# A convolution-attention-expert kernel: a first block that loads and normalises one channel tile ahead of the other, a seam with operations issued in another order, and two stores from another queue

## The chip, the cores and the metric

The kernel runs on one core of a Trainium2 chip. The metric is the device time of one execution in microseconds; the kernel before took 1997.98 us as the median of three runs (1995.13 to 2001.15). One further execution was profiled and took 1985.54 us. Engines have short names: PE is TensorE (PEld its weight loads), DVE is VectorE, ACT is ScalarE, POOL is GpSimd and SP is SyncE, which only issues transfers. A name with a q behind it (ACTq, SPq) is an engine's sequencer, which issues the DMAs.

## The reference

Two images of 256 channels and 56x56 pixels go through two layers; cut to what matters:

```python
# layer 0
y = einsum('oc,bchw->bohw', w_qkv1, group_norm(x))        # 768 output channels
y = conv_general_dilated(y, w_qkv2, (1, 1), 'SAME', feature_group_count=768)   # 3x3, each channel alone
q, k, v = split(y)                                         # 8 heads of 32 channels
for s in (0, 1):                                           # 4 heads each, 7x7 window, dilation 1 and 2
    attn = softmax(q * scale . k over the window + rpb[s]) # bias by relative position
    outs[s] = attn . v
x = x + w_proj . concat(outs)
# layer 1, on 6272 tokens of 256
t = t + linear_attention(layer_norm(t))                    # elu+1 features, then a feed-forward block
t = t + experts(layer_norm(t))                             # top 2 of 8 experts, hidden 1024, gelu
```

group_norm takes mean and variance over 8 channels and all pixels, so no product can be scaled before a whole channel tile has been counted. 128 channels are one tile; x has two (ct 0 and ct 1), which are the two halves of the contraction of w_qkv1.

## The kernel before, in words

The work is a sequence of stages, each of which mixes two kinds of work, so that PE has something to do while the other waits.

- 0 to about 435 us: the convolutions of image 0 and its attention (`first_image`, L1064). `Convolutions.run` (L504) goes through six blocks of 128 output channels, each in two halves of 28 rows (hf 0 and 1). For each half: PE multiplies (`py`, L529, four row groups, two channel tiles each), ACT copies into a padded tile `ypad` (L535), and the 3x3 convolution follows. PE takes 8 of the 28 rows as nine diagonal matmuls (`pc`, L550). For the other 20 rows ACT does the first of nine taps (L569) and DVE the eight others (L579). The result `yc` lies in one of two buffers, and is stored to DRAM as `yd` (L587), from where the attention loads it again (`ld`, `v`).
- The head of that stage, the first 20 us: `load_x` (L462) loads x in four column pieces per channel tile, `norm_image` (L469) counts all of it (`bn_stats`, L478), adds up over groups with a small matmul by `g8` (`gps`), forms the scale with a power on POOL (L151), and DVE scales x in place (L499).
- Beside it `bias_tables` (L363) builds the attention's tables of exp(bias): a cleared tile `pf` is written to DRAM (`frame`), the biases are turned there element by element (`turned`, L374), put into the frame (L379), read back as `pf` (L383), ACT takes Exp (L387), POOL multiplies with masks (L405) and writes `fp`, from which the attention loads its tables `tab` (L714).
- 435 to about 746 us: the convolutions of image 1 as filling for half 0 of layer 1's linear attention (`linear`, L1659): `keys` (L267), then queries, messages, feed-forward and routing in an order of PE written out by hand.
- From about 746 us, the seam: the attention of image 1 begins, with the expert tiles of half 0 (`Experts.run`, L1601) as its filling. Before it, the last tokens of half 0 are stored (`store`, L1996) and routed: `weights` (L2033) takes an Exp on ACT, DVE finds slots (`chosen`, `before`, `slot`), POOL scatters token rows into `xs`. In the attention, `settle` (L772) copies transposed keys and queries (qT0, qT1, kT0, kT1) out of PSUM, `scores` (L641) takes Exp on ACT and multiplies it by a table on DVE, and `values` (L660) multiplies by v on PE. An expert tile gathers its tokens (`xr<-xs`, L1544), and `weigh` (L1567) forms their weights `eq` on DVE. `LEAD` is the number of steps by which the filling starts ahead.
- After about 1030 us: linear attention of half 1, then experts alone, with PE nearly always busy, to the end.

Every engine runs its instructions in order. A scheduler orders them from priorities and an estimate of when their inputs come; `tc.issue_after(x)` keeps an instruction behind x in that order, `tc.high_priority` moves it ahead, and `tc.manual_schedule` keeps the order as written for the engines it names. `anchors` is a dictionary of instructions that such orders refer to. Since one moved instruction shifts those around it, the order of every engine differs between the two kernels far behind the changed lines.

## Time and profile before

| | us |
|---|---|
| median of three runs | 1997.98 (1995.13 to 2001.15) |
| the profiled execution | 1985.54 |
| its span, first to last instruction | 1983.8 |
| PE busy | 1840.1 (93%) |
| DVE busy | 1093.3 (55%) |
| ACT busy | 705.8 (36%) |
| POOL busy | 578.8 (29%) |
| PE busy from 0 to 30, 30 to 75, 75 to 435 | 12.68, 42.68, 329.82 |
| PE busy from 435 to 746, 746 to 800, 800 to 1030 | 287.88, 40.10, 213.12 |
| PE busy from 1030 to 1960, 1960 to 1984 | 907.14, 6.66 |

The mean granted clock of PE is 0.972 of full speed; from 746 to 800 us it is 0.62. A line of the timeline in the next section reads: start, duration, engine, line of the kernel, operation, output<-inputs, shapes, count, and in brackets the idle time of the engine before it and what ended that.

### The profile page before, as it was taken

The numbers are of one execution on the slowest core, as the hardware profiler recorded it, in microseconds if no ns is written. First come the engines' busy times: TensorE is split into PE (matmuls) and PEld (weight loads), VectorE is DVE, ScalarE is ACT, GpSimd is POOL, SyncE is SP. The second block draws the span as 40 slices with busy tenths as digits, with TensorE's granted clock in tenths as the row PEclk, the third lists the DMA queues.
The fourth block names the chain that finished last, engine by engine and source line by source line (L and its number), as shares of the span: only waits on it lengthen the run. The fifth ranks groups of instructions, "written<-read, shape, count | busy, mean of one in ns | idle before, by whom it ended". The sixth has DMA issues, their size and how long they took to land.

```text
span 1983.8 us, 27692 instructions
## 1 busy us (share of the span) xinstructions
PE 1840.1 (93%) x9996; PEld 1304.7 (66%) x9996; DVE 1093.3 (55%) x2728; ACT 705.8 (36%) x1337; POOL 578.8 (29%) x634
## 2 busy tenths in 40 slices
PE   6999899988989997999989989999999999999996
PEld 3444454556645564665668755668788888888885
DVE  6887988889888546555557434655622222222121
ACT  2233324334434223544536543323322222222332
POOL 4520042025202444111126311345422323222221
PEclk9999999999989996999999999999999999999998
DMA  4644422350003334754464210114677676767995
GB/s 113 152 114 128 152 75 84 101 151 35 25 33 94 107 85 140 205 153 137 130 191 126 72 35 32 46 62 133 182 227 198 185 201 186 200 190 197 299 279 166
DMA packets 200147, 268.79 MB, mean 135 GB/s; under 512 B 30952, under 2 KB 158614, under 8 KB 199760
## 3 DMA queue, kind: packets, MB, share of 16 engines
q1 hardware_dynamic: 167920, 223.95, 37.4%
q0 software_dynamic: 19728, 27.54, 7.4%
q10 hardware_dynamic: 12352, 15.43, 2.3%
q8 instruction: 81, 1.33, 0.3%
q14 instruction: 66, 0.54, 0.1%
HBM read 200.19 MB, written 70.95 MB: 137 GB/s over the span
## 4 chain that ended last, share of the span: by engine, by line
PE 48%; DMA 5%; DVE 3%; ACT 3%; issue 1%; SPq 0%; POOL 0%; ACTq 0%; DVEq 0%; POOLq 0%
PE ph L1617 13%; PE py L1637 13%; PE p L1961 4%; DMA xr<-xs 2%; PE x L1637 2%; PE py L1977 2%; PE x L1617 2%; DMA xs<-in_c_fill 2%; PE po L666 2%; PE pm L1931 1%; PE kx L317 1%; PE x L359 1%; PE kp L305 1%; PE pq L1888 1%; PE px L1584 1%; PE s_ps L652 1%
## 5 line engine op out<-in xcount | busy, mean ns | idle before, releaser
L1617 PE MATMUL ph<-xe,w1e 128*128 128x256 f32 (+1 forms) x1448 | 309.2, 369 | 10.6 <-ACT hT L1621 4.1
L1637 PE MATMUL py<-w2e,hT 128*128 128x256 f32 x1392 | 311.3, 379 | 0.0
L1621 ACT ACTIVATE hT<-ph,sv 128x256 f32<-128x256 f32 (+1 forms) x362 | 165.7, 462 | 387.3 <-PE ph L1617 384.2
L1617 PEld LDWEIGHTS ph<-xe,w1e 128*128 128x128 f32 x1448 | 261.2, 190 | 49.8 <-ACT hT L1621 6.1
L1637 PEld LDWEIGHTS py<-w2e,hT 128*128 128x128 f32 x1392 | 260.1, 190 | 33.1 <-issue 0.2
L168 POOL DMA_INDIRECT y<-yt,idi x101 | 160.2, 1587 | 322.6 <-DVE yt L1643 178.2
L579 DVE SCALAR_TENSOR_TENSOR yc<-ypad,w,yc 128x1120 f32<-128x1120 f32 x144 | 202.5, 1410 | 31.4 <-ACT yc L569 29.0
L262 POOL TENSOR_TENSOR rs<-rs,mhalf 128x2 f32<-128x2 f32 (+3 forms) x90 | 72.8, 812 | 325.4 <-DVE rs L261 277.6
L529 PE MATMUL py<-x_sb,wq 128*128 128x448 f32 (+1 forms) x384 | 155.9, 538 | 8.3 <-ACT ypad L535 4.4
L656 ACT ACTIVATE p<-s_ps 112x952 f32<-112x952 f32 (+5 forms) x88 | 102.1, 1160 | 150.6 <-PE s_ps L652 101.4
L1574 DVE CAST idi<-xr 128x2 int32<-128x2 f32 (+1 forms) x53 | 10.9, 205 | 255.9 <-DMA xr<-xs 255.9
L657 DVE TENSOR_TENSOR p<-p,tab 112x952 f32<-112x952 f32 (+5 forms) x88 | 122.0, 1389 | 47.4 <-ACT p L656 47.3
L550 PE MATMUL pc<-ypad,diag 128*128 128x448 f32 x324 | 131.4, 547 | 0.0
L1643 DVE SCALAR_TENSOR_TENSOR yt<-py,eq,yt 128x256 f32<-128x256 f32 x87 | 41.7, 482 | 156.3 <-PE py L1637 156.1
L1599 POOL TENSOR_SCALAR yt<-b2e,eq 128x256 f32<-128x256 f32 x101 | 50.7, 507 | 257.6 <-DMA b2e<-in_L_ffn_b 198.6
L529 PEld LDWEIGHTS py<-x_sb,wq 128*128 128x128 f32 x384 | 72.2, 199 | 71.4 <-issue 55.7
L168 POOL DMA_INDIRECT xs<-row,si x98 | 97.5, 995 | 64.4 <-DVE si L2108 34.7
L572 DVE SCALAR_TENSOR_TENSOR yc<-ypad,w,yc 128x784 f32<-128x784 f32 x96 | 104.9, 1114 | 1.3 <-ACT yc L569 0.9
L666 PE MATMUL po<-p,v 98*32 98x170 f32 (+5 forms) x960 | 70.8, 376 | 28.6 <-DVE p L657 15.3
L550 PEld LDWEIGHTS pc<-ypad,diag 128*128 128x128 f32 x324 | 60.0, 191 | 52.3 <-issue 48.5
L1961 PE MATMUL p<-xT,fw 128*128 128x512 f32 (+1 forms) x208 | 93.6, 573 | 0.0
L1961 PE MATMUL p<-m2T,fw 128*128 128x512 f32 (+2 forms) x224 | 93.4, 539 | 0.0
(394 smaller groups left out, 2883.8 us busy)
## 6 DMA issues: line engine op xcount, KB each, us to landing
w1e<-in_L_ffn_W SPq DMA_DIRECT2D x53, 1024.0 KB
w2e<-in_L_ffn_W SPq DMA_DIRECT2D x53, 1024.0 KB
yd<-yc SPq DMA_DIRECT2D x24, 784.0 KB
ld<-yd SPq DMA_DIRECT2D x28, 448.0 KB
xr<-xs SPq DMA_DIRECT2D x48, 260.0 KB
b2e<-in_L_ffn_b SPq DMA_DIRECT2D x53, 128.0 KB
t<-td SPq DMA_DIRECT2D x12, 512.0 KB
y<-t ACTq DMA_DIRECT2D x24, 256.0 KB
```

What stands on the lines that cost most here:

```text
L168: ins = nc.gpsimd.indirect_dma_start(out=dst[:, :], out_offset=bass.IndirectOffsetOnAxis(ap=index, axis=0), in_=src, in_offset=None, **kw,)
L529: nc.tensor.matmul(py[:, :n, :], self.wq1[:, ct, oc * P : (oc + 1) * P], self.x_sb[:, ct, (q0 + g0) * WW : (q0 + g0 + n) * WW], start=(ct ...
L550: nc.tensor.matmul(pc, diag[:, tap, :], ypad[:, dy : dy + SHARE, dx : dx + WW], start=(tap == 0), stop=(tap == 8),)
L572: nc.vector.scalar_tensor_tensor(yc[:, y0:y1, :], src, w, yc[:, y0:y1, :], ALU.mult, ALU.add)
L579: nc.vector.scalar_tensor_tensor(yc[:, y0:y1, :], src, w, yc[:, y0:y1, :], ALU.mult, ALU.add)
L656: nc.scalar.activation(p[:nk, :, :n], s_ps[:nk, :, :n], AF.Exp)
L657: nc.vector.tensor_tensor(grid(p), grid(p), table[:nk], ALU.mult)
L666: nc.tensor.matmul(dst[hs] if w is None else den[hs], v[:nk, hs] if w is None else w[:nk, :], p[:, h, :, o : o + q.shape[2]], start=first ...
L1617: nc.tensor.matmul(p1, x.w1[:, ct, j * P : (j + 1) * P], x.xe[:, ct, :], start=(ct == 0), stop=(ct == 1),)
L1621: newest[3] = nc.scalar.activation(hT[:, j, :], p1, AF.Gelu, bias=x.sv[:, 4 + j : 5 + j]).ins
L1637: nc.tensor.matmul(py, hT[:, j, h * P : (h + 1) * P], x.w2[:, j, :], start=(j == 0), stop=(j == NJ - 1),)
L1961: nc.tensor.matmul(p1[:, :w], fw1[:, k, oc * P : (oc + 1) * P], rhs, start=(k == 0), stop=(k == 3))
```

## The change

It has three parts.

Head. A new function `first_block` takes the place of `load_x` and `norm_image` for image 0. x is loaded with all pieces of channel tile 0 first, from both queues in turn; after it come g8 and the first 128 columns of the weight, then channel tile 1; the rest of the weight comes later, from ACT's queue. Each channel tile is counted, normalised and scaled by itself, and the products of tile 0 for six of eight row groups are made while tile 1 is counted; they are kept in PSUM banks of the attention. The order on PE and DVE is written out there. The clearing of pf, and with it the writes of `frame` and `turned`, wait for the second statistic of channel tile 1; the loads of masks and of the projection weight come behind them.

Seam. In `keys` the addition of b2 on POOL is always made, and no longer in `message`. The weighing of an expert tile is put behind the newest multiplication by a table. The stores of tokens and the Exp in `weights` of half 0 are put behind the copies of kT1 of the attention's first group. `LEAD` goes from 22 to 24.

Stores. The two stores of `yc` of image 0, output block 1, are issued by ACT instead of SP.

```diff
-LEAD = 22
+LEAD = 24
...
-        if b2 is not None:
-            nc.gpsimd.tensor_tensor(t, t, b2[p].unsqueeze(1).to_broadcast([rows, n, C]), ALU.add)
+        nc.gpsimd.tensor_tensor(t, t, b2[p].unsqueeze(1).to_broadcast([rows, n, C]), ALU.add)
...
-            nc.vector.memset(pf, 0.0)
+            with tc.issue_after(anchors["counted"]), tc.high_priority():
+                nc.vector.memset(pf, 0.0)
...
-            nc.sync.dma_start(frame.rearrange("h r c -> (h r) c"), pf)
+            ld = nc.sync.dma_start(frame.rearrange("h r c -> (h r) c"), pf)
+            anchors.setdefault("framed", ld.ins)
...
-            with nc.allow_non_contiguous_dma(reason="676 values"):
+            with tc.issue_after(anchors["framed"]), nc.allow_non_contiguous_dma(reason="676 values"):
...
-            self.load_x(0)
             self.g8 = self.cw.tile([P, P], F32, name="g8")
-            nc.scalar.dma_start(self.g8, a["c_g8"])
+            self.wq1 = self.cw.tile([P, 2, 3 * C], F32, name="wq1")
+            wq1 = a["w_qkv1_t"].rearrange("(ct p) o -> p ct o", p=P)
+            for ct in range(2):
+                for k, (c0, c1) in enumerate(zip((0, G, 3 * G, 5 * G), (G, 3 * G, 5 * G, T))):
+                    eng = nc.scalar if k % 2 else nc.sync
+                    eng.dma_start(self.x_sb[:, ct, c0:c1], xv[0, :, ct, c0:c1])
+                if ct == 0:
+                    nc.scalar.dma_start(self.g8, a["c_g8"])
+                    nc.sync.dma_start(self.wq1[:, :, :P], wq1[:, :, :P])
...
+            nc.scalar.dma_start(self.wq1[:, :, P:], wq1[:, :, P:])
...
+        def first_block(self, att):
...
+            def mean(ct):
+                nc.vector.bn_aggr(mv[:, ct, :], st[:, ct, :, :].rearrange("p g s -> p (g s)"))
+                nc.tensor.matmul(gps[ct][:, 0:1], self.g8, mv[:, ct, 0:1], start=True, stop=True)
+                gm, dv = gms[ct], dvs[ct]
+                nc.vector.tensor_copy(gm, gps[ct][:, 0:1])
+                nc.vector.tensor_tensor(dv, mv[:, ct, 0:1], gm, ALU.subtract)
+                nc.vector.tensor_tensor(dv, dv, dv, ALU.mult)
+                nc.vector.tensor_tensor(dv, dv, mv[:, ct, 1:2], ALU.add)
...
+            with tc.manual_schedule(engines={mybir.EngineType.PE, mybir.EngineType.DVE}):
+                count(0, *range(NG))
+                mean(0)
+                variance(0)
+                count(1, 0)
+                scaled(0, 0, G)
+                products(0, 0)
+                count(1, 1)
+                scaled(0, G, T // 2)
+                products(0, 1)
+                count(1, *range(2, NG))
+                mean(1)
+                scaled(0, T // 2, T)
+                products(0, 2)
+                variance(1)
+                products(0, 3, 4, 5)
+                scaled(1, 0, G)
+                products(1, 0)
+                scaled(1, G, T // 2)
+                products(1, 1, 2)
+                scaled(1, T // 2, T)
+                products(1, 3, 4, 5)
...
-                    st = nc.sync.dma_start(
+                    st = (nc.scalar if (b, oc) == (0, 1) else nc.sync).dma_start(
...
-            nc.vector.tensor_tensor(grid(p), grid(p), table[:nk], ALU.mult)
+            anchors["scaled"] = nc.vector.tensor_tensor(grid(p), grid(p), table[:nk], ALU.mult).ins
...
+                                if banks and g == 0:
+                                    anchors["settled"] = ins.ins
...
-        next(tables)
         for k, (b, done) in enumerate(run):
+            if k == 0:
+                next(tables)
+                with tc.issue_after(anchors["framed"]):
+                    att.load_projection()
...
-                self.weigh(x)
+                with tc.issue_after(anchors["scaled"]):
+                    self.weigh(x)
...
-                if half == 0:
-                    tt = tk.at(n0 + k0, 2)
-                    nc.gpsimd.tensor_tensor(tt, tt, b2.unsqueeze(1).to_broadcast([P, 2, C]), ALU.add)
...
+        def behind():
+
+            turned = run == 0 and half == 0 and "settled" in anchors
+            return tc.issue_after(anchors["settled"]) if turned else nullcontext()
...
-                ins = nc.scalar.dma_start(
-                    y2[(n0 + k0) * P : (n0 + k0 + kn) * P, :].rearrange("(n p) c -> p n c", p=P),
-                    tk.at(n0 + k0, kn),
-                )
+                with behind():
+                    ins = nc.scalar.dma_start(
+                        y2[(n0 + k0) * P : (n0 + k0 + kn) * P, :].rearrange("(n p) c -> p n c", p=P),
+                        tk.at(n0 + k0, kn),
+                    )
...
-            with tc.issue_after(newest[3]) if half and newest[3] is not None else nullcontext():
+            with tc.issue_after(newest[3]) if half and newest[3] is not None else behind():
                 nc.scalar.activation(ms[1], ms[1], AF.Exp)
...
-                            tk, wk, sm, ps_a, bank, w_k, b2 if half or pairs[j][1] == 1 else None, kx, acc, *pairs[j], j == 0, j == len(pairs) - 1, j < 3 and half == 0
+                            tk, wk, sm, ps_a, bank, w_k, b2, kx, acc, *pairs[j], j == 0, j == len(pairs) - 1, j < 3 and half == 0
```

## The prediction

> **What bounds the kernel now.** I read the page first: its busy times and its chain.
>
> ```profile
> PE 1840.1 (93%) x9996; PEld 1304.7 (66%) x9996; DVE 1093.3 (55%) x2728; ACT 705.8 (36%) x1337; POOL 578.8 (29%) x634
> ...
> PE 48%; DMA 5%; DVE 3%; ACT 3%; issue 1%; SPq 0%; POOL 0%; ACTq 0%; DVEq 0%; POOLq 0%
> ```
>
> TensorE is busy for 1840.1 of 1983.8 us, so 143.7 us of it are gaps, and only these, or matmuls run at a low clock, can be won. The change touches the first 100 us and the seam near 750 us; so next the busy time of windows around the seam (columns: span, then busy time and count of PE, PEld, DVE, ACT, POOL, then granted clock, DMA share, GB/s):
>
> ```profile
> 735.00:747.00 12.00, 12.00 (x73) 8.32 (x63) 4.10 (x18) 3.19 (x11) 6.20 (x7) 1.00 0.47 126
> 747.00:760.00 13.00, 7.93 (x44) 6.14 (x42) 10.12 (x63) 4.78 (x17) 4.51 (x5) 0.63 0.28 79
> ...
> 781.00:798.00 17.00, 9.42 (x53) 4.97 (x56) 7.63 (x18) 4.61 (x7) 4.99 (x7) 0.60 0.79 271
> ```
>
> PE goes from fully busy to 61% and 55%, at a clock of 0.6. Then the timeline, for who releases whom. The head:
>
> ```profile
> 4.59 1.15 DVE L478 BATCH_NORM_STATS2 st<-x_sb 128x6 f32<-128x448 f32 x2 [3.58 <-DMA x_sb<-in_x]
> ...
> 9.89 1.03 SPq L374 DMA_DIRECT2D turned<-in_L_conv_rpb  x1
> 11.10 3.26 DVE L478 BATCH_NORM_STATS2 st<-x_sb 128x6 f32<-128x448 f32 x6 [1.11 <-DMA x_sb<-in_x]
> ...
> 17.92 4.50 DVE L499 TENSOR_SCALAR x_sb<-x_sb,gm,rs_gn 128x448 f32<-128x448 f32 x6 [0.85 <-POOL rs_gn L151]
> 18.49 8.14 PE L529 MATMUL py<-x_sb,wq 128*128 128x448 f32 x16 [1.62 <-DVE x_sb L499]
> ...
> 24.75 7.86 SPq L379 DMA_DIRECT2D frame<-turned  x2
> ...
> 28.41 11.33 DVE L579 SCALAR_TENSOR_TENSOR yc<-ypad,w,yc 128x1120 f32<-128x1120 f32 x8 [5.99 <-ACT yc L569]
> ...
> 33.60 2.38 SPq L383 DMA_DIRECT2D pf<-frame  x2
> ...
> 39.18 0.35 ACT L387 ACTIVATE pf<-pf 84x33 f32<-84x33 f32 x2
> ```
>
> Nothing multiplies before 18.49: x arrives until 11.1, then come statistics, normalisation, scaling. From 28.41 DVE runs taps almost without a pause to 68.05, so a later or earlier first tap carries on to there. The bias tables wait for two slow writes (the first is issued at 9.89, its reader leaves at 24.75). Times at which a transfer landed, here and below, are the ends of its packets in the trace's DMA records. The block that the third part moves:
>
> ```profile
> 72.19 1.23 ACT L569 ACTIVATE yc<-ypad,w 128x1120 f32<-128x1120 f32 x1 [8.46 <-DMA yd<-yc]
> ...
> 75.33 0.53 SPq L587 DMA_DIRECT2D yd<-yc  x1
> ...
> 81.45 1.23 ACT L569 ACTIVATE yc<-ypad,w 128x1120 f32<-128x1120 f32 x1 [1.21 <-DMA yd<-yc]
> ...
> 84.96 0.34 SPq L587 DMA_DIRECT2D yd<-yc  x1
> ```
>
> Two buffers hold yc; a new block waits until an old one is stored. The store issued at 75.33 could have gone when its taps ended (68.05), but stood behind table stores and loads on SP. The seam:
>
> ```profile
> 750.70 0.20 ACT L2037 ACTIVATE m<-m 128x4 f32<-128x4 f32 x1 [3.99 <-DVE m L2096]
> ...
> 751.39 1.75 PE L767 MATMUL x<-ident,ld 112*128 112x112 f32 x8 [3.76 <-ACT qT L776]
> ...
> 753.02 0.64 PE L2099 MATMUL x<-chosen,tri 128*128 128x32 f32 x2
> ...
> 786.37 0.23 DVE L1572 TENSOR_SCALAR eq<-xr,etmA 128x2 f32<-128x2 f32 x1 [5.72 <-DMA xr<-xs]
> ...
> 788.51 1.16 PE L666 MATMUL po<-p,v 112*32 112x280 f32 x8 [6.77 <-DVE p L657]
> ...
> 793.54 2.93 PE L1617 MATMUL x<-xe,w1e 128*128 128x256 f32 x6 [0.81 <-DVE xe L1587]
> ```
>
> Two gaps, 3.76 and 6.77 us. In the second, DVE stands in the expert weight eq, waiting for gathered tokens, while a finished softmax tile waits behind it for its table.
>
> **Part 1, the head.** Channel tile 0 of x comes first. All x lands from 4.6 to 11.6; at that pace half is there near 7.7. Its seven statistics (14 took 1.15+3.42+3.26 = 7.8, so 0.56 each) end at about 9.2. From the end of the aggregates to the first scaling took 17.92 - 14.81 = 3.1; so tile 0 is scaled from about 12.5 (9.2 + 0.26 + 3.1). DVE then has seven statistics (3.9) and two of the three scalings of tile 0 (1.1 of half of 4.50): 17.5. A second norm, 0.3 + 3.1, puts the scaling of tile 1 at 21.0 to 23.3. Scaling alone ends 0.9 later than before (22.42), but PE has done tile 0's six products by then; only the four of tile 1 in the first half remain for the first convolution, of which the last needs rows beyond column 1568, so it starts after 23.3. Its copy ends near 24.9 instead of 27.05; with the other copies and the 1.23 of ACT's first tap DVE starts its taps at 26.7, not 28.41: -1.7 (-0.5 to -3).
>
> Against it: the clearing of pf, and so both slow writes, wait for a statistic that ends near 13.6; they leave at 14.1 and 15.5 instead of 9.89 and 12.11. In the trace they landed at 24.68 and 31.95, so the second took 7.3 alone, the first 14.8 beside the loads of x and weights. At 7.1 to 7.3 each, the second lands at 28.5 to 32.6, and pf (5.25 after it, as in 31.95 to 37.20) at 34 to 37.9; I take 36.3. Exp of pf ran at 39.18 though pf was there at 37.20; it now stands earlier in ACT's order, and ACT waits for it from about 34, up to 2.9, with the next first tap behind it and DVE behind that; POOL's table work then starts 2 to 3 before 39.50, and the stores that fill the queue ahead of 72.19 move with it. I take -3 at 72 (from 0 to -5): the two effects overlap, they do not add. The other moved loads (projection, far, masks, rest of the weight) have no reader before 39; the weight's rest is read after 40; they cost nothing while the DMAs idle from 24 to 40 (16 us, 13 GB/s); without that cover 1 MB costs 2.5 at the 410 GB/s of the start.
>
> **Part 2, the seam.** First gap: ACT no longer stands in the store and Exp (3.99) before its copies, so the first transposes go through. But the next PE step, the counts from chosen at 753.02, needs DVE results that end at 752.9 and are not touched. In the new order the second strip's first transposes share one PSUM bank with the counts and wait for DVE's slot (755.55 to 755.73), where they had run at 753.95; and the copy of kT for the first strip falls behind stores on ACT. Then 1.0 transposes, 0.5 copy, 1.0, 0.6 copies, 0.2 and 0.3 for the logits, 2.0 transposes: 755.7 + 5.6 = 761.3 for the first scores against 759.18: +2.1, or 0 if DVE's slot comes sooner. I take +1.2.
>
> Second gap: eq moves behind the table multiplies. Twenty-four matmuls (16 of values, 8 of scores) that stood behind the wait run in it: at 0.6 to 0.75 per eight 2.0. The expert's products wait for their weights, which landed at 790.17, instead of 793.54: 3.4. Together -5.3, at most 6.77, at least -2 (the matmuls alone). b2's adds: twelve of 1.3 on POOL, which already ran between 436 and 500: 0, within ±1. LEAD, 22 to 24 steps: 0.
>
> The rows show that the clock falls after these gaps: 0.63 and 0.60 in the windows quoted, 1.00 before. [...]
>
> **Part 3, the stores.** SP is spared 0.53 + 0.34 = 0.87 of issue. On ACT each store stands ahead of the next first tap (in the new order the second store is directly before it). The store waits for eight DVE taps; the tap for the next buffer, done at 82.68 before DVE was free (84.85), now begins after: DVE idles 0.4 + 1.23 = 1.6. For the first store no such wait, and it leaves up to 7.3 sooner (75.33 to 68.05), which can end the 1.21 wait at 81.45; SP's table loads and tokens also come sooner, and half of a PE gap of 2.45 at 95.10 may close. 0, from -2 to +2. [...]
>
> **Sum.** -3 + 1.2 - 5.3 + 0 = -7.1. The profiled execution took 1985.54 (1.7 outside its span), 12.4 below the median of 1997.98; I subtract from both alike: 1978 of such an execution, 1991 as median. Bounds: -5 - 6.8 - 2 = -13.8, and 0 + 2.1 - 2 + 2 = +2.1; every engine's order is also reshuffled behind the change (some 10000 order lines on DVE), for which I add ±5. That gives 1979 to 2005.
>
> **Rivals.** (a) The gains are hidden: the tables land at 37.9, which leaves 0 of the head, and the pause before the weights takes the place of the 6.77, which leaves -2; with +1.2, -0.8: 1997. For it: weights land at 790.17 whatever DVE does.
> (b) ScalarE's queue in order makes it slower. If the slow writes keep their old 14.8 and 19.8 us, the second lands at 35.3, pf at 40.6, Exp ends at 41. DVE has six taps of 1.42 from 26.7, to 35.2, then idles until a first tap ends at 42.6: 7.4, of which 1.7 is the head's own gain: +5.7. The same queueing costs 1.6 twice at the stores and 2.1 at the seam: +11, with the second gap still won at half (-2 to -5.3): +6 to +9, 2005. It decides when pf lands after 38. Against it: the writes' 7.3 alone.
> (c) The slot comes early, the clock stays up and both waits vanish: -13.8, 1984.
>
> Chances: forecast 0.42, (c) 0.10, (a) 0.20, (b) 0.28. What can be told from no change is about 0.3%, 6 us. Faster: 0.10 and most of the forecast, 0.38, so 0.48; slower 0.27; same 0.25. The range goes from 1979 to 2008 to take in most of (b).
>
> **What will show it.** First taps on DVE near 26.7; pf's Exp before 38 with less than 3 of waiting; the wait of 8.46 shorter. DVE's wait for xr after the last table multiply, no gap over 4 on PE at 781 to 790, and the expert's first product near 790. First scores between 759 and 761. Wrong if Exp waits over 4, if DVE idles at each store on ACT, or if a later stage, 800 to 1030 above all, lost time in the new order.

## The result and the profile after

The changed kernel took 1991.88 us (median of 12 runs, 1986.80 to 1997.96) beside 1998.17 for the kernel before (12 runs, 1990.86 to 2001.27). The ratio is 0.9977, with a 95% interval from 0.9965 to 0.9988: 4.6 us less, by the interval 2.4 to 7.0. (The quotient of the two medians is 0.9969; here and below the ratio, with its interval, is what counts.) It is a gain, but a smaller one than the 7.1 us of the sum, and by itself inside the 0.3% that the prediction called hard to tell from no change.

The page of the changed kernel: busy times, then the shares of the chain that ended last.

```profile
PE 1836.9 (92%) x10000; PEld 1300.9 (65%) x10000; DVE 1092.1 (55%) x2733; ACT 703.3 (35%) x1335; POOL 575.2 (29%) x635
...
PE 67%; DVE 15%; DMA 7%; ACT 5%; issue 3%; POOL 2%; SPq 0%; ACTq 0%; DVEq 0%; POOLq 0%
```

TensorE does the same work in a span of 1988.5 us, 4.7 longer than the span of the trace before, although the median is lower. The two traces were not taken under like conditions: the kernel before took 1984 us on two chips of this study, 1992 on a third and 1997 on a fourth; its trace (1985.5) fits the first two, and the 1998 beside the result fits the fourth. So I read from the traces who waits for whom, and from times taken side by side on one chip what an edit is worth.

The head, in the timeline of the changed kernel (start, duration, engine, line, what, and in brackets the idle time ahead of it and who ended that):

```profile
21.65 2.46 DVE L549 TENSOR_SCALAR x_sb<-x_sb,gm,rs_gn 128x448 f32<-128x448 f32 x3 [0.67 <-POOL rs_gn L151]
21.85 3.06 PE L583 MATMUL po<-x_sb,wq 128*128 128x448 f32 x4
24.74 2.89 PE L583 MATMUL s_ps<-x_sb,wq 128*128 128x448 f32 x8
...
27.67 1.70 ACT L615 COPY ypad<-s_ps 128x448 f32<-128x448 f32 x4 [17.60 <-PE s_ps L583]
...
30.96 8.49 DVE L659 SCALAR_TENSOR_TENSOR yc<-ypad,w,yc 128x1120 f32<-128x1120 f32 x6 [6.84 <-ACT yc L649]
...
38.95 0.23 ACT L388 ACTIVATE pf<-pf 84x33 f32<-84x33 f32 x1
39.37 0.23 ACT L388 ACTIVATE pf<-pf 84x33 f32<-84x33 f32 x1 [0.19 <-DMA pf<-frame]
...
72.63 1.23 ACT L649 ACTIVATE yc<-ypad,w 128x1120 f32<-128x1120 f32 x1 [9.27 <-DMA yd<-yc]
```

Tile 1 is scaled from 21.65, but PE still owes products of tile 0 (two matmuls to a product): four matmuls, for two row groups of the second half, run from 21.85 to 24.9 at 0.77 us each, while the eight behind them take 0.36 each; the granted clock is recorded as 0.5 from 21.22 to 24.64 and as 1.0 after. The first copy therefore starts at 27.67, and DVE's first tap at 30.96: 2.55 later than before, where 1.7 earlier was forecast. The copies add to it. Before, they followed PE one at a time, the first and the last of the four at:

```profile
21.88 0.53 ACT L535 COPY ypad<-py 128x448 f32<-128x448 f32 x1 [13.04 <-PE py L529]
...
26.66 0.39 ACT L535 COPY ypad<-py 128x280 f32<-128x280 f32 x1 [0.41 <-PE py L529]
```

Now all four start behind the last of the eight matmuls, though the products of the first row group ended at 25.66: the four lie in one tile (`s_ps`). That the shared tile is the reason is read from the code and these times; no run splits it. Exp of the tables runs at the old time, and the wait for a stored buffer at 72 us is 9.27 instead of 8.46: the store that ends it leaves SP at 61.06, where it had left at 59.99.

The seam of the changed kernel by windows, the last of them one that the prediction showed of before (columns as there):

```profile
746.00:760.00 14.00, 7.79 (x36) 5.50 (x37) 7.65 (x45) 3.22 (x12) 8.47 (x9) 0.50 0.80 231
760.00:781.00 21.00, 15.15 (x117) 7.79 (x116) 13.15 (x59) 5.93 (x10) 7.78 (x9) 0.50 0.84 193
781.00:798.00 17.00, 14.29 (x114) 7.45 (x111) 9.30 (x21) 5.78 (x8) 5.30 (x8) 0.66 0.74 250
```

The first two of these windows before the change:

```profile
746.00:760.00 14.00, 8.93 (x62) 6.88 (x61) 11.05 (x69) 5.25 (x19) 4.51 (x5) 0.66 0.30 87
760.00:781.00 21.00, 19.75 (x164) 11.23 (x161) 16.24 (x73) 8.06 (x14) 13.56 (x14) 0.58 0.45 138
```

The stretch from 781 to 798, where the gap of 6.77 had been, gained 14.29 - 9.42 = 4.87 us of PE work. The two ahead of it lost 1.14 and 4.60, at a clock of 0.50 and a DMA share of 0.8 where it had been 0.30 and 0.45. (The windows lie at the same times in both, while this execution was 5.5 us ahead at 740, so they don't hold the same work.) What moved the transfers is the next view, the changed kernel's timeline on PE, DVE and SP's queue:

```profile
744.05 5.47 SPq L1063 DMA_DIRECT2D v<-yd  x7
750.07 0.81 SPq L884 DMA_DIRECT2D ld<-yd  x2
750.93 20.96 SPq L792 DMA_DIRECT2D tab<-fp  x15
771.99 0.96 SPq L884 DMA_DIRECT2D ld<-yd  x2
...
756.04 0.98 PE L730 MATMUL s_ps<-qT,kT 32*112 32x187 f32 x8
...
776.83 0.64 PE L845 MATMUL x<-ident,ld 112*128 112x112 f32 x2 [1.29 <-DMA ld<-yd]
779.24 0.64 PE L845 MATMUL x<-ident,ld 112*128 112x112 f32 x2 [1.77 <-DMA ld<-yd]
...
793.71 0.23 DVE L1655 TENSOR_SCALAR eq<-xr,etmA 128x2 f32<-128x2 f32 x1
...
796.72 1.99 PE L1701 MATMUL x<-xe,w1e 128*128 128x256 f32 x8
```

Before, seven table loads stood in this place and the next `ld` went out at 765.81:

```profile
747.80 8.79 SPq L714 DMA_DIRECT2D tab<-fp  x7
765.81 0.84 SPq L804 DMA_DIRECT2D ld<-yd  x2
```

Now fifteen are issued in one run, 21 us long, and `ld` leaves at 771.99 although this execution was 5.5 us ahead at 740. The transposes that read it wait, 1.29 and 1.77 us. In the same place ACT stands 5.30 us before 778.31 for something that the trace can only call remote; more of this below.

### The profile page after: what moved, and what is told of

Same layout as the page of the kernel before. It is cut to its first block, busy times and chain, and to the rows that moved or that the text cites. A ratio compares the mean times of both kernels' runs of the same rounds, so it can differ in the third digit from the quotient of the medians.

```text
span 1988.5 us, 27707 instructions
## 1 busy us (share of the span) xinstructions
PE 1836.9 (92%) x10000; PEld 1300.9 (65%) x10000; DVE 1092.1 (55%) x2733; ACT 703.3 (35%) x1335; POOL 575.2 (29%) x635
## 4 chain that ended last, share of the span: by engine, by line
PE 67%; DVE 15%; DMA 7%; ACT 5%; issue 3%; POOL 2%; SPq 0%; ACTq 0%; DVEq 0%; POOLq 0%
PE py L1721 13%; PE ph L1701 13%; PE p L2042 7%; PE pc L630 4%; PE po L744 4%; DVE yc L659 4%; PE py L583 3%; PE py L2058 3%; PE x L1721 3%; DVE yc L652 2%; PE s_ps L730 2%; PE x L1701 2%; DMA xs<-in_c_fill 2%; DMA xr<-xs 2%; PE pq L1972 1%
## 5 line engine op out<-in xcount | busy, mean ns | idle before, releaser
L1701 PE MATMUL ph<-xe,w1e 128*128 128x256 f32 (+1 forms) x1464 | 313.6, 370 | 10.5 <-ACT hT L1705 7.5
L1701 PEld LDWEIGHTS ph<-xe,w1e 128*128 128x128 f32 x1464 | 265.3, 191 | 48.3 <-ACT hT L1705 9.1
L583 PE MATMUL py<-x_sb,wq 128*128 128x448 f32 (+1 forms) x360 | 141.6, 523 | 8.8 <-ACT ypad L615 5.6
L583 PEld LDWEIGHTS py<-x_sb,wq 128*128 128x128 f32 x360 | 65.4, 193 | 67.4 <-issue 49.0
```

The costliest lines, as they stand in the source:

```text
L583: nc.tensor.matmul(py[:, :n, :], self.wq1[:, ct, oc * P : (oc + 1) * P], self.x_sb[:, ct, q0 * WW : (q0 + n) * WW], start=(ct == 0), stop= ...
L1701: nc.tensor.matmul(p1, x.w1[:, ct, j * P : (j + 1) * P], x.xe[:, ct, :], start=(ct == 0), stop=(ct == 1),)
```

## Experiments

The runs fell on four chips, on which the kernel before took 1984.3 us (head, seam and stores alone), 1984.7 (pieces of the seam), 1997.2 (the second look at the change, `no_lead`, `head_fixed`) and 1992.0 (the last run). Each ratio is against the kernel before on the same chip.

### The three parts, each alone

Head alone, into the kernel before:

```diff
-            self.load_x(0)
...
-            for _ in self.norm_image():
-                pass
+            self.first_block(att)
...
+            with tc.issue_after(anchors["counted"]), tc.high_priority():
+                nc.vector.memset(pf, 0.0)
```

> The head alone. As predicted: first DVE tap near 26.7 and about 3 us ahead at 72; time -3 (ratio 0.9985). Theory 2, from the trace of the changed kernel: the copies of the four row groups wait for one PSUM tile whose last product ends at 27.6, the first tap is 2.5 us later than before (30.9 against 28.4), the tables arrive at the same time, and at 72 nothing is won: -0.4 there; time 0 within 2 (0.999 to 1.001). Theory 3: the reordering behind the head is what brings the changed kernel 4 us ahead at 300 to 435; then this kernel shows these 4 us there.

Measured: 0.9996 [0.9982, 1.0010], 1984.11 beside 1984.3. The trace has the same head as the changed kernel's: copies from 26.81, first tap at 30.10, Exp at 38.75 and 39.45, and 9.63 of waiting for the stored buffer at 72.68. The head is worth nothing that the times can tell: between -3.6 and +2.0 us. The 4 us ahead at 300 to 435 of theory 3 are in this trace (3.4, as a median of starts against the first trace before), but as much in `stores_only` and `weigh_only` (3.6 each), so they aren't the head's.

Seam alone:

```diff
-LEAD = 22
+LEAD = 24
...
+                with tc.issue_after(anchors["scaled"]):
+                    self.weigh(x)
...
+                with behind():
+                    ins = nc.scalar.dma_start(
```

> The seam alone. As predicted: first scores +1.2 and the gap of 6.8 us gone, -4 in all (0.998), and nothing different before 430 us. Theory 2: the stores of tokens put behind the copies of kT1 move eleven loads of v ahead of fifteen table loads on SP's queue, where they wait until about 741; the tables then load during the seam, 750 to 772, and the strip's tokens behind them: 5 to 6 us lost between 747 and 784, 8 to 10 won after, in all -3 to -5 at 800 against 740; time -1 to -5.

Measured: 0.9982 [0.9968, 0.9997], 1981.51 us: -3.6 us, by the interval -0.6 to -6.4. It is the one of the three whose interval leaves out no change.

Stores alone:

```diff
-                    st = nc.sync.dma_start(
+                    st = (nc.scalar if (b, oc) == (0, 1) else nc.sync).dma_start(
```

> The two stores of the second block alone, issued by ACT. As predicted: DVE idles 1.6 us where the second store stands ahead of the first tap, what SP gains pays for it: 0 within 2 us (0.999 to 1.001). Theory 3: the gain of 4 us at 300 to 435 comes from here, since SP's loads of v, tokens and tables go out sooner: -4 at 350 (0.998). Rival: ACT's queue is held up: +2 to +4 at 120.

Measured: 0.9997 [0.9979, 1.0014], 1985.92 us: nothing, between -4.2 and +2.8 us. The first store leaves at 67.82 instead of 75.33, right behind its taps as the prediction had it, and the wait of 1.21 us that this could end, at 81.45, is down to 0.03 at 82.52. The longer wait, 9.71 at 73.16, is for an earlier store, which SP still issues at 59.86. DVE doesn't idle for the second store here, since the tap for the next buffer stands ahead of that store in ACT's order, other than in the changed kernel.

### The kernel before once more

Nothing is edited. The question was whether PE's stalls of 3 to 4.5 us between 1300 and 1400, which the changed kernel's trace has and the trace before has not, come and go with the execution.

> The kernel before once more, for a second trace of it. Theory A (the profiled execution of before, 1985.5, was a lucky one; its luck lies between 1300 and 1400 us, where the changed kernel's trace has two PE gaps of 3.5 and 4.5 us behind the ACT activation hT and loses 12.4 us): the new trace has such gaps there too, and its execution is near 1995 to 1998. Theory B (the loss at 1300 to 1400 is the changed order's own): the new trace has no PE gap over 2 us there and again ends near 1985.

Measured: 1990.97 us, so between the two theories' times. Neither stall is in its trace. For the one of 3.5 us this says that it goes with the changed order (`lead_only` below has it). For the second, in the changed kernel's trace

```profile
1366.29 3.56 PE L1701 MATMUL ph<-xe,w1e 128*128 128x256 f32 x8 [4.48 <-ACT hT L1705]
```

it decides nothing, since this run fell on a chip where the kernel before takes 1984 us; see `after_again`. And this execution of the same program ended 5.4 us later than the first: at 740 the two are 0.0 apart, at 880 to 920 3.6, at 1250 to 1300 6.1. Single executions vary by as much as the change is worth.

### The pieces of the seam, each alone

Weighing behind the newest table multiply:

```diff
+            anchors["scaled"] = nc.vector.tensor_tensor(grid(p), grid(p), table[:nk], ALU.mult).ins
...
+                with tc.issue_after(anchors["scaled"]):
+                    self.weigh(x)
```

> Of the seam, only the weighing behind the table multiplies; PE's order is that of before, so PE still meets the expert's transposes after the same sixteen value matmuls. As predicted: DVE's wait of 5.7 us and PE's gap of 6.8 us go, -3 to -5 between 780 and 800, 0 elsewhere (ratio 0.998). Theory 2 (it is LEAD that moves 24 matmuls ahead of the expert's): of the gap only the wait behind eq goes, PE then waits for the tokens and weights instead: -1 to -3 at 800, and nothing that a time can tell (0.999 to 1.000).

Measured: 0.9960 [0.9944, 0.9975], 1977.73 us. PE's timeline, and `eq` on DVE in the second fence:

```profile
783.25 1.08 PE L1584 MATMUL x<-ident,xr 128*128 128x128 f32 x4 [3.96 <-DMA xr<-xs]
784.27 1.15 PE L652 MATMUL s_ps<-qT,kT 32*112 32x238 f32 x8
788.27 3.75 PE L1618 MATMUL x<-xe,w1e 128*128 128x256 f32 x8 [2.85 <-DMA w1e<-in_L_ffn_W]
```

```profile
785.29 0.22 DVE L1572 TENSOR_SCALAR eq<-xr,etmA 128x2 f32<-128x2 f32 x1
```

DVE no longer stands in `eq`. PE does: its order is unchanged, the expert's transposes still come next, and they wait for the gathered tokens themselves. The gap of 6.77 falls into 3.9 and 2.8, the second of which ends with the expert's weights.

The filling two steps further ahead:

```diff
-LEAD = 22
+LEAD = 24
```

> Of the seam, only LEAD 24 instead of 22. As predicted: 0. Theory 2: LEAD is what moves expert matmuls behind two more strips of attention, so the gap of 6.8 us is filled and -5 to -8 stands at 810; it is also the only edit that reorders PE up to the end of half 1, so the two gaps of 3.5 and 4.5 us at 1320 to 1400 and their +6 to +7 come from here; in all -1 to -3 (0.999).

Measured: 0.9983 [0.9972, 0.9994], 1981.11 us. This is the edit that reorders PE. Around the first expert tile the two orders differ like this (minus is before):

```
 L666 Matmult po<-p,v x4
 L666 Matmult po<-p,ones x4
-L1584 Matmult x<-ident,xr x4
 L652 Matmult s_ps<-qT,kT x4
-L1617 Matmult x<-xe,w1e x4
 L666 Matmult po<-p,v x4
 L666 Matmult po<-p,ones x4
-L1617 Matmult x<-xe,w1e x4
+L1584 Matmult x<-ident,xr x4
```

The gap stays, as DVE still stands in `eq` ahead of the multiply that PE needs; PE's line and the two of DVE and PE near it:

```profile
779.53 1.16 PE L666 MATMUL po<-p,v 112*32 112x280 f32 x8 [6.38 <-DVE p L657]
```

```profile
777.62 0.23 DVE L1572 TENSOR_SCALAR eq<-xr,etmA 128x2 f32<-128x2 f32 x1 [5.13 <-DMA xr<-xs]
```

So in these traces the gap needs both edits: the weighing out of DVE's way, and LEAD to take the transposes out of PE's. (It is gone with LEAD 22 too in `no_lead` below, but there PE came so late that the tokens were there.) The new order also has a price, in the profile of the same run:

```profile
1325.21 2.03 PE L1888 MATMUL pq<-xT_ab,w_q 128*128 128x128 f32 x8 [3.50 <-ACT hT L1621]
```

Token stores and Exp behind the copies of kT1:

```diff
+                with behind():
+                    ins = nc.scalar.dma_start(
...
-            with tc.issue_after(newest[3]) if half and newest[3] is not None else nullcontext():
+            with tc.issue_after(newest[3]) if half and newest[3] is not None else behind():
```

> Of the seam, only the stores of tokens and the Exp behind the copies of kT1; PE's order is that of before, SP has eleven loads of v ahead of fifteen table loads. As predicted: the gap of 3.8 us goes, the first scores come +1.2 later. Theory 2: the tables load between 750 and 772 with the DMAs busy, the next tokens behind them: +5 to +6 at 780, which the expert part does not give back; time +4 to +6 (1.002 to 1.003).

Measured: 0.9975 [0.9960, 0.9989], 1979.97 us. PE, then SP's queue:

```profile
748.49 0.63 PE L2107 MATMUL x<-chosen,tri 128*128 128x32 f32 x2 [2.39 <-ACT kT L792]
752.39 1.01 PE L767 MATMUL x<-ident,ld 112*128 112x112 f32 x4 [2.10 <-DVE slot L2110]
...
778.76 0.63 PE L767 MATMUL x<-ident,ld 112*128 112x112 f32 x2 [6.29 <-DMA ld<-yd]
```

```profile
746.19 5.47 SPq L985 DMA_DIRECT2D v<-yd  x7
752.71 0.82 SPq L806 DMA_DIRECT2D ld<-yd  x2
753.57 19.74 SPq L714 DMA_DIRECT2D tab<-fp  x15
773.42 0.97 SPq L806 DMA_DIRECT2D ld<-yd  x2
```

The gap of 3.76 at 747 becomes one of 2.4 and one of 2.1, and a new one of 6.3 stands at 772, on `ld`. This edit alone reorders SP: eleven loads of v come ahead of two `ld` and all fifteen tables. SP waits until 743 at the fourth of those v loads, so the tables that had gone out before pile up behind them.

### The changed kernel without the moved token stores

The Exp stays behind the copies; the stores go back.

```diff
-                with behind():
-                    ins = nc.scalar.dma_start(
+                ins = nc.scalar.dma_start(
```

> The changed kernel, with the stores of tokens where they were before (the Exp stays behind the copies). As predicted: about the changed kernel's time. Theory 2: SP's queue has the table loads early again, and the 5 to 6 us lost from 747 to 784 come back: -4 to -6 against the changed kernel, 0.995 to 0.996 against before. Rival: the gap of 3.8 us at 747 returns, since ACT stands in the store again: +1 to +2 against the changed kernel.

Measured: 0.9948 [0.9933, 0.9963], 1975.71 us beside 1984.7, on the chip of the pieces. SP's queue is as it was before the change:

```profile
745.10 8.77 SPq L792 DMA_DIRECT2D tab<-fp  x7
762.86 0.83 SPq L884 DMA_DIRECT2D ld<-yd  x2
```

Neither the gap on `ld` nor the one of 6.77 is left on PE; the longest from 744 to 800 us is one of 3.42 on ACT's first copies, which was 3.76 before. The stall of 3.50 after 1321 is there.

The same kernel on another chip, since its relatives gained less elsewhere (below):

> The changed kernel with the token stores back at their old place, the same program as the earlier run (ratio 0.9948 [0.9933, 0.9963], 1975.7 us beside a before of 1984.7). Theory A, the gain is the program's: the ratio is again between 0.993 and 0.9965, wherever the kernel before stands (about 1974 beside 1984, about 1987 beside 1997); the seam has no stall of PE over 4 us between 745 and 800 us, and the one of 3.5 us near 1321 to 1332 us is there. Theory B, the second order of half 1 costs more where the kernel before takes about 1997: there the ratio is 0.9965 to 0.998, and a stall of 3 to 4.5 us near 1360 us is there beside the first. If the kernel before takes about 1984 again, theory B is not tested.

Measured: 0.9981 [0.9969, 0.9993], 1989.03 beside 1992.02. The gain is not the program's alone: the medians are 9.0 us apart on the one chip and 3.0 on the other (10.3 and 3.8 by the ratios), and the intervals do not meet. Theory A fails; of theory B the stall near 1360 is there (4.05 before 1363.03), the ratio lies just above its range. Here the seam has stalls that the first run lacked. PE, ACT, DVE and SP's queue in the slower run:

```profile
764.32 0.81 SPq L884 DMA_DIRECT2D ld<-yd  x2
764.37 0.25 ACT L183 COPY kT<-x 128x112 f32<-128x112 f32 x1 [3.79 <-remote]
764.65 0.28 DVE L185 COPY kT<-x 128x112 f32<-128x112 f32 x1 [4.04 <-ACT kT L183]
...
766.37 0.57 PE L1478 MATMUL x<-cnt,ones 128*128 128x8 f32 x2 [6.25 <-DVE cnt L2181]
```

and the copy of the same name in the faster run:

```profile
763.24 0.25 ACT L183 COPY kT<-x 128x112 f32<-128x112 f32 x1 [1.71 <-PE x L845]
```

In the faster run ACT copies as soon as PE's transposes are done. In the slower one it stands for 3.8 us for something that the trace can only call remote, DVE behind it, and PE for 6.25 behind both.

### The change on the slower chip, and two variants

The changed kernel, unedited:

> The changed kernel once more, for a second trace and for times beside the two below. Theory 2: the two 6 us effects in the seam (tables loaded at 751 to 772, no gap at 782) repeat; the PE gap of 3.5 us near 1325 repeats, since LEAD's order makes it, and the one of 4.5 us at 1362, which no other kernel with LEAD 24 shows, does not; time 0.997 to 0.998.

Measured: 0.9967 [0.9952, 0.9982], 1990.15 beside 1997.23. The first result is repeated; -6.6 us here, -4.6 there. In the trace the run of fifteen table loads repeats (750 to 769) and so does the stall of 3.5 us (before 1335.59). Two signs fail. PE has a gap of 4.12 us before 784.75, where none was expected, behind DVE, which stands there for something remote. And the second stall, which was not to repeat, does: 3.22 us before 1370.80. It is in all five traces from the slower chips (2.87 to 4.48 us, with LEAD 24 or 22); in those from the faster ones nothing over 1.3 us stands in its place. So it goes with the chip and not with the change.

Token stores early and LEAD as before:

```diff
-LEAD = 24
+LEAD = 22
...
-                with behind():
-                    ins = nc.scalar.dma_start(
+                ins = nc.scalar.dma_start(
```

> The changed kernel with LEAD 22 and the stores of tokens where they were before. If LEAD is a gain in the seam and a loss at 1320 to 1400 of nearly the same size: PE waits again for tokens and weights at 780 to 790 (3.9 and 2.8 us, as with the weighing alone), no gap of 3.5 us near 1325, and the time is within 2 us of the kernel that differs by LEAD alone (0.9948): 0.994 to 0.996. If LEAD is worth the 3 us that it showed alone: 0.996 to 0.997.

Measured: 0.9961 [0.9946, 0.9975], 1990.02 us. The stall of 3.5 near 1325 is gone, and the time is that of the change (1990.15 on this chip): within the whole change no gain by LEAD is shown. The waits of 3.9 and 2.8 that were expected at 780 to 790 don't come. PE is held up before, 5.58 us until 768.92, the tokens are there when their transposes come, and only 1.73 us of waiting for the weights are left, before 793.89. The ratio is between the two of the kernel that differs by LEAD alone (0.9948 and 0.9981, each on another chip), so it doesn't decide between the two expectations. It has the stall of 2.87 at 1352.86 that the runs on the faster chips lack.

Token stores early, and the head mended: the bias tables' writes no longer wait for a statistic, and the products of rows behind the first half come last.

```diff
-            with tc.issue_after(anchors["counted"]), tc.high_priority():
-                nc.vector.memset(pf, 0.0)
+            nc.vector.memset(pf, 0.0)
...
-                products(0, 3, 4, 5)
+                products(0, 3)
...
-                products(1, 3, 4, 5)
+                products(1, 3)
+                products(0, 4, 5)
+                products(1, 4, 5)
```

> The changed kernel with the stores of tokens early, and in the head two things turned: the products of the last two row groups come after those of the first half, and pf is cleared at the start, so that the slow writes leave as soon as x is issued. Theory 2 (the head won nothing because PE's backlog at half clock held the four copies, and because the tables came no earlier): copies from about 24.6 instead of 27.7, the first DVE tap near 28 instead of 31, pf's Exp 4 us sooner, and 3 us ahead at 72; time -3 against the same kernel without these two (0.9948): 0.993 to 0.994. Rival: the writes beside x's load slow x, and the wait at 72 is for another transfer: 0.

Measured: 0.9982 [0.9967, 0.9997], 1995.04 us. The first copies start only 0.7 sooner, at 26.94, and the first tap is no sooner. Its timeline:

```profile
22.07 1.70 PE L584 MATMUL py<-x_sb,wq 128*128 128x448 f32 x2
...
29.95 0.53 ACT L616 COPY ypad<-po 128x448 f32<-128x448 f32 x1 [1.31 <-PE po L584]
31.64 11.98 DVE L660 SCALAR_TENSOR_TENSOR yc<-ypad,w,yc 128x1120 f32<-128x1120 f32 x8 [7.67 <-ACT yc L650]
...
38.84 0.35 ACT L387 ACTIVATE pf<-pf 84x33 f32<-84x33 f32 x2
...
67.24 1.23 ACT L650 ACTIVATE yc<-ypad,w 128x1120 f32<-128x1120 f32 x1 [3.84 <-DMA yd<-yc]
```

So the edit did half of what it was to do: another product of tile 0 (`py`, two matmuls at 0.85 us each) slipped into the place of the two that were moved back, and in ACT's order a copy of the second half, whose product now comes late, stands ahead of the first tap. The tables are back by 36.6 us, and Exp still runs at 38.84, behind copies in ACT's order.

The block that had waited until 72.6 starts at 67.24, 5 us sooner. That can't be put down to the head: this start moves as much in programs whose order is that of the kernel before until the seam. It is 72.19 and 73.51 in the two traces before, 68.67 in `lead_only`, and in `weigh_only`, where the store that it waits for landed 7 us after its issue and not 12:

```profile
65.29 1.23 ACT L569 ACTIVATE yc<-ypad,w 128x1120 f32<-128x1120 f32 x1 [1.86 <-DMA yd<-yc]
```

Whether a head without PE's backlog would win is thus not tested.

### All traces side by side

For every instruction that a trace shares with the first trace before, I took the difference of the starts; the table has their medians in five stretches (us, negative is earlier). The programs of `seam_only`, `weigh_only`, `settled_only` and `lead_only` have the order of the kernel before on every engine until the seam, so the row for 700 to 740 is no effect of theirs; what matters is how a column changes from there. In the row for 778 to 784 the engines lie apart (in `settled_only` DVE's additions are 4.7 later, PE's products 5.9 to 7.4, POOL's scatters 3.0 earlier), so its medians are rough.

```
stretch      before  weigh  settled lead   seam   tokens  after  after  no_    tokens_early
             again   only   only    only   only   early          again  lead   again
 700-740       0.0   -4.2    -3.4   -8.6   -5.6   -2.7    -5.5   -5.5   -5.0   -7.7
 778-784       0.0   -4.2    +4.7   -8.6   +1.0   -2.4    +5.6   +5.1   +4.0   +1.3
 820-840      +0.5   -4.8    -3.6  -12.7  -10.9  -12.5    -5.2   -4.4   +0.8   -8.4
1250-1300     +6.1   -5.3    -2.5  -14.2  -13.3  -14.4    -7.0   -4.2   +0.4  -10.5
1600-1800     +4.8   -6.0    -3.0   -6.0   -6.7   -3.9    +5.4   +8.4   +5.9   +3.7
```

Three things can be read. First, with the token stores moved (`settled_only`, `seam_only`) 8.1 and 6.6 us are lost from 740 to 784 and given back, or more, by 840; with them early, on the chip of `settled_only` (`tokens_early`), there is no loss. Second, each kernel with LEAD 24 loses 7 to 14 us from 1300 to 1600. Not all of it is a loss: at the same hidden-layer copies near 1300 these kernels have run 656 of the expert tiles' products, and `weigh_only`, `no_lead` and the kernel before 672; the sixteen that are owed take 3.8 us (eight took 1.89). The stall is 3.5, and the clock of 0.91 and 0.96 in `lead_only`, where it is 1.00 before, costs up to 20 x 0.09 + 40 x 0.04 = 3.4 (windows 1320 to 1340 and 1360 to 1400). That is 10.7 against the 8.2 of its column. Third, the traces taken where the kernel before needs over 1990 (`after`, `after_again`, `no_lead`, `tokens_early_again`, and `head_fixed`, from +1.4 to +11.9) all lose 10.4 to 13.9 between 740 and 1600, whichever edits they have; on the faster chips the most is the 4.8 of the kernel before itself. These five have pieces of all three parts of the change in them, so the chip is told from the program by one pair alone: the kernel of `tokens_early`, which wins 1.1 there in the first trace and loses 11.4 in the second.

## Why the prediction was right, and where it was not

The time was forecast as 1991, within 1979 to 2008, and came to 1991.9 beside a kernel before at 1998.2. The sum gave -7.1, the two comparisons -4.6 and -6.6. The direction and the place of the gain, the seam, were right; that the sum came out near is in part luck, since the head's 3 us did not come, and the seam's forecast left out what LEAD does, both ways, and the loads on SP. By its terms:

- **Head, -3: wrong, it is 0.** The step that failed is "PE has done tile 0's six products by then". I had priced the counts and scalings of DVE and no product; at 0.77 us each PE was still at tile 0 when tile 1 was scaled, and ACT's first copy began at 27.67, where the forecast had a copy end near 24.9. That figure also took three of the four copies as done by then, and the trace has all four behind the last product, 1.70 us. The bias tables were late too: the slow writes took 10.9 and 8.1 us (15.35 to 26.22, to 34.30), not 7.1 to 7.3 each, and pf came back at 38.9 and 39.35 where I took 36.3. That is past the 38 from which rival (b) was to decide, but its 7.4 us of waiting did not come: ACT was busy with copies until then and DVE idled 1.31 at 40.75. `head_only` puts a bound of -3.6 to +2.0 on all of it. The -3 at 72 could not have been read from one trace: without any edit there, that wait ends anywhere from 65.3 to 73.5.
- **First scores, +1.2: too small.** 756.04 is 3.1 earlier than 759.18 in an execution that was 5.5 ahead, so +2.3, just over the upper bound of 2.1. The larger price of the move was elsewhere. I had listed the engines that a delayed store passes and not what SP's queue does when the stores' position shifts the scheduler's order of loads: eleven v loads ahead of fifteen tables, and `ld` 6 to 8 us late.
- **Second gap, -5.3: the gap went, by two edits and not one.** "Eq moves behind the table multiplies. Twenty-four matmuls that stood behind the wait run in it" is the step that failed. Without LEAD the matmuls that could run are not next in PE's order; the transposes are, and they wait 3.96. LEAD, priced at 0, put the twenty-four there. With both, the longest gap left on PE from 781 to 798 is one of 1.68 before 792.84. The expert's first product, forecast near 790, came at 796.72 (790.97 in `seam_only`): 4.87 us of work won in that stretch were 5.74 lost in the two ahead of it.
- **LEAD, 0: wrong in mechanism and price.** In the pieces it is needed for the gap, and it costs a stall of 3.5 and some clock (0.91 and 0.96 in `lead_only`) in a stage 550 us later, for which the prediction had named only "a later stage" as a danger. Alone it is worth -1.2 to -5.6; what it is worth inside the change is open.
- **b2, 0: not tested alone**, but nothing speaks against it: in `seam_only`, which has it, POOL's operations come in the old order until 815 us.
- **Stores, 0: right.** The working behind it holds in the changed kernel, where DVE idles 1.79 at 87.02 for the second store and 1.6 was forecast; in `stores_only` that idling is missing, and the first store's gain is there.

The seam as a whole was forecast at -4.1 and measured at -3.6 alone; what was mis-sized in the total is the head. In the trace of `seam_only` that -3.6 is made otherwise than forecast: 5.3 us are won from 740 to 840 and 4.2 given back by 1600 to 1800, where the kernels with LEAD 24 lose. Which of the pieces carry the seam's gain is not settled: alone they took -7.9 (-5.0 to -11.1), -5.0 (-2.2 to -7.9) and -3.4 (-1.2 to -5.6), and together, on another chip, -3.6. They may be in each other's way, the table loads and LEAD's later stall being what the traces show of it, or the chip may make the difference, as it did for one program above (0.9948 and 0.9981). For the pieces alone the traces fall short of the times: behind 740, `weigh_only` wins 1.8 and `settled_only` nothing. A single execution varies by more than that.

Rival (a), hidden gains and 1997, was right for the head. For the seam it had the right next wait, the expert's weights: 2.85 in `weigh_only`, none once LEAD is there.

The version without the moved token stores is ahead of both kernels on one chip (0.9948) and level with the change on another (0.9981 beside 0.9977 and 0.9967). What makes the difference between the chips was not found.

## What to carry to other kernels

A wait can stand in two orders at once: to run work inside it, look at the order of the engine that waits and at that of the engine that would do the work, and move both (with only DVE's order moved PE still waited 3.96 and 2.85 us here, with only PE's 6.38). When a transfer is held back, read the whole queue of every issuing engine in the new order, because a load that waits for a buffer can hold those behind it: in `settled_only` SP stood at loads of v until 743 us, fifteen tables went out behind them from 753.57 to 773.31, and `ld` at 773.42. And price the products of a reordered head, not only the statistics: here the four matmuls of the second half ran at 0.77 us each, at a granted clock of 0.50 to 24.64, and DVE's first tap came 2.55 us later than before.

## What the runs showed of the hardware

**The granted clock differed between two traces in which PE idled as long.** The windows from 540 to 555 and 570 to 585 us of the kernel before, then of `stores_only`, whose order there is the same but which is 2 to 3 us ahead:

```profile
540.00:555.00 15.00, 12.28 (x30) 6.10 (x28) 11.81 (x16) 5.98 (x13) 1.41 (x1) 0.77 0.13 54
...
570.00:585.00 15.00, 13.28 (x33) 5.83 (x32) 14.55 (x23) 3.30 (x6) 0.00 (x0) 0.89 0.13 55
```

```profile
540.00:555.00 15.00, 11.47 (x31) 5.50 (x30) 13.10 (x22) 7.51 (x14) 0.00 (x0) 0.89 0.13 54
...
570.00:585.00 15.00, 13.31 (x31) 5.91 (x32) 15.00 (x23) 3.86 (x6) 0.00 (x0) 1.00 0.13 55
```

PE idles 6.69 of the 60 us from 540 to 600 in both (in the trace before the longest gaps are 1.21, 1.44 and 1.09 us), and the granted clock (third number from the end) is 0.77 and 0.89 in the one, 0.89 and 1.00 in the other. By 600 us the second is 2.6 us further ahead. In the clock's records of the kernel before, all 33 changes of the granted clock lie on one grid of 3.41 us, and so do the 31 in the changed kernel's trace, whose grid, counted from the first instruction, lies 1.2 us further on (borders at 74.59 and at 21.22 us). The gaps of 1.09 and 0.63 us ahead of 576.4 fall into one step of the trace before (1.7 us idle of 3.41), and the clock is 0.5 for the next step; in `stores_only` it is 1.00 from 570 to 585. That the place of the gaps on such a grid makes this difference is my reading, and no run shows it. In the trace before, the clock fell here with no gap of PE over 1.5 us. In the seam of the changed kernel it was 0.50 from 746 to 781 us with no gap over 2.4, PE being 56% and 72% busy.

**The same kernel took 1984 to 1998 us on different chips**, and the traces from the slower ones have stalls that the others lack, the longest (4.9 to 6.9 us) between 778 and 792 us, with ACT, DVE and sometimes PE idle together and the wait put down to "remote" (for one Exp of ACT 6.85 us in `no_lead`, 6.09 in `head_fixed`, 5.30 in the changed kernel). No such line is in any trace from the two faster chips, or in the first one before. The 10.4 to 13.9 us that every trace from a slower chip loses behind 740 are of the size of the difference between the chips; that they are its cause is inferred, as the kernel before was not traced there.
